# Ranks with layer 0's rows, later layers addressed by rank, one rare branch, two parts per chunk: a four-layer graph network on one core

## The chip, the core and the metric

The kernel runs on one core of one Trainium2 chip. The core has five engines with a queue of instructions each: PE (TensorE, matmuls), DVE (VectorE), ACT (ScalarE), POOL (GpSimd) and SP (SyncE, which issues DMAs); 16 DMA engines move the data that SP and POOL ask for. POOL issues all indirect DMAs: gathers of rows by a column of indices, and scatters. The metric is the device time of one launch in microseconds. Before the change three runs took 5230.04, 5248.34 and 5253.61 us.

## What is computed

3125 nodes of 128 values, 100,000 edges (sorted by destination), and four graph layers, each followed by a residual and a layer norm. Cut to what matters:

```python
x = _layernorm(x + _L0_gnn_ref(x, L0_gnn_z, edge_index, edge_type_500, ...))
x = _layernorm(x + _L1_gnn_ref(x, edge_index, ...))
x = _layernorm(x + _L2_gnn_ref(x, edge_index, edge_attr_3, ...))
x = _layernorm(x + _L3_gnn_ref(x, edge_index, edge_type_8, node_type_4, ...))

# layer 0: attention over edges and the node itself; relation rows z of 500 types
pre_edge = hP1[dst] + hP2[src] + zP3[edge_type]
logit_edge = _leaky(pre_edge) @ y_w
t_edge = hWh[src] + zWz[edge_type]           # weighed by the softmax, summed per dst
# layer 1: mean of neighbours, two matmuls with a relu
# layer 2: softmax over the edges of a node, with a bias from edge_attr
attn = jnp.sum(Q[dst] * K[src], axis=-1) * SCALE + edge_bias
attn_exp = jnp.exp(attn - jnp.max(attn))     # one maximum over all edges
attn_norm = attn_exp / jnp.maximum(attn_sum[dst], 1e-12)
agg = jax.ops.segment_sum(V[src] * attn_norm[:, :, None], dst, num_segments=n)
# layer 3: keys and values by node type, turned by a matrix per edge type (8)
scores = jnp.sum(q_dst * k_t, axis=-1) / scale * mu[edge_type]
out = jax.ops.segment_sum(V[src] * softmax(scores), dst)
```

## The kernel before

**Tiles and slots.** Nodes are padded to 3200 and ranked by falling in-degree (the matmuls `keep`, L325, sort them); tile t holds the 128 nodes of ranks 128t to 128t+127, one to a partition. Each node's incoming edges are its slots; tile t has CAP[t] slots, 57 for the first, 21 for the last, 821 in all. A gather (`gather`, L101) fetches one row per partition: the source node's row for one slot. Slots are worked in chunks of W = 8, 114 chunks in all. Edges beyond CAP are left to `behind` (L773): a `For` loop with `rounds` trips, which is zero trips for these inputs; the function stands ahead of layers 0, 2 and 3.

**Tables in DRAM.** h_tab holds layer 0's rows (1056 bytes, written by 25 stores in order of nodes), kv_tab layer 2's keys and values (1 KB), xq_tab the residual x and query, ktv_tab layer 3's rows, 8 KB a node: one key-value pair for each of 8 edge types. h_tab, kv_tab and ktv_tab lie by node number, xq_tab by rank. A slot's index into the first two is its source's number (`srcx`), into ktv_tab source x 8 + edge type (`idx`, made from `pay[:, :, 2]`).

**Layer 0** is placed by a planner: flows of steps, one per kind of work, are put in an order on each engine. Per chunk, eight gathers bring `hs`; PE transposes and multiplies, ACT applies a relu, DVE sums the logits (L1359) and does the softmax. **Layer 1** multiplies by a table of edge counts on PE, and at its end writes, for each tile j, the rows of kv_tab by a plain store on SP (L1571) and those of xq_tab by a scatter on POOL (L1572).

**Layers 2 and 3** share `passes` (L1678). A beat handles one chunk: the key product of the new chunk (`keyed`, L1593), the weighing of one earlier chunk whose softmax is done, a "part" (`weighed`, L1600), the reduction of the scores (L1596), and the sum over the slots of the part weighed one beat before (`summed`, L1604), which is then added to `accb`. Between these come `lanes.slot()` calls, which run one step each of side lanes: the softmax chain, the closing of a finished tile, the making of its rows, and their put. The order in which the code is written is the order on each engine. In layer 2 a closed tile goes through the output matmuls and yields its 8 KB rows for layer 3 (L1866), which `put3` scatters to ktv_tab by POOL (L104). After the last tile `few` counts the softmax sums that are too small under the global maximum; a branch (L1981) works them anew, which these inputs don't take. Layer 3 begins with memsets of m, l and accb (L2003 to L2006) and its own `behind3`.

Of the kernel before, what the change touches and what calls it, by code (L numbers as in the profile page):

```python
# [9 lines left out]
F32 = mybir.dt.float32  # L10
F16 = mybir.dt.float16
BF16 = mybir.dt.bfloat16
I32 = mybir.dt.int32
# [23 lines left out]
HC = 2 * D + H  # L37
NK = (PADREL + 1) // P
# [48 lines left out]
def tile_gnn(ctx, tc, a, out):  # L87
# [34 lines left out]
    upper = const.tile([P, P], F32, name="upper")  # L122
# [4 lines left out]
    before = const.tile([P, SUP * P], BF16, name="before")  # L127
# [117 lines left out]
    def edge_table(key, unsorted, payload, between):  # L245
# [6 lines left out]
        with tc.tile_pool(name="key_d", bufs=1) as kp, tc.tile_pool(name="kw_d", bufs=3) as kw, \  # L252
# [47 lines left out]
            V.tensor_copy(ranki, rank)  # L300
            rlo = kp.tile([P, NT], I32, name="rlo")
# [45 lines left out]
    h_tab = dram.tile([NP, HC], F32, name="h_tab")  # L347
# [15 lines left out]
    def tables(tp, ps):  # L363
# [12 lines left out]
        def table(src, n, width, w, dst, parts=None):  # L376
            for r in range(0, dst.shape[0], P):
# [13 lines left out]
                if parts is not None:  # L391
                    V.tensor_copy(h[:, HC:], xt)
                    rest = tp.tile([P, R], F32, name="rest")
                    for i in range(3):
                        p = parts[:, r // P, i * R:(i + 1) * R]
                        V.tensor_copy(p, xt if i == 0 else rest)
                        if i < 2:
                            V.tensor_sub(rest, xt if i == 0 else rest, p)
                nc.sync.dma_start(dst[r:r + P], h[:, :dst.shape[1]])
# [4 lines left out]
    with tc.tile_pool(name="edges", bufs=1) as ep:  # L404
# [24 lines left out]
        V.scalar_tensor_tensor(pay[:, :, 2], src, float(NET), et8, op0=OP.mult, op1=OP.add)  # L429
# [456 lines left out]
    with tc.tile_pool(name="l0", bufs=2) as wp, tc.tile_pool(name="l0s", bufs=1) as sp, \  # L886
# [92 lines left out]
        def with_z(hs, s0, k, zs):  # L979
            V.tensor_add(hs[:, s0:s0 + k], hs[:, s0:s0 + k], zs[:, :k, :HC])  # L980
# [20 lines left out]
        def behind0(t, pl, mk, rl):  # L1001
# [3 lines left out]
            hs = wp.tile([P, W, HC], F32, name="hs", bufs=8)  # L1005
# [14 lines left out]
            V.tensor_add(lg, lg_ps, hs[:, :, 2 * D:])  # L1020
# [186 lines left out]
        def flow_rows(k):  # L1207

            yield from hss.take()
            k.hs = wp.tile([P, W, HC], F32, name="hs", bufs=8)  # L1210
# [112 lines left out]
        def add_t(k, s0, n, t_ps):  # L1323
            while k.rows <= (s0 + n - 1) // 4:
                yield 0.5
            V.tensor_add(k.hs[:, s0:s0 + n, D:], k.hs[:, s0:s0 + n, D:], t_ps[:, :n])  # L1326
# [22 lines left out]
        def flow_lg(k):  # L1349
# [9 lines left out]
            V.tensor_add(run.lg[:, at:at + k.w], lg_at[:, run.k % 2, at:at + k.w], k.hs[:, :k.w, 2 * D:])  # L1359
# [81 lines left out]
    with ExitStack() as ctx1, tc.tile_pool(name="l1", bufs=2) as wp, tc.tile_pool(name="l1s", bufs=1) as sp:  # L1441
# [92 lines left out]
        with tc.tile_pool(name="l1pay", bufs=1) as pp:  # L1534
            pays = pp.tile([P, NS, PW], I32, name="pays")
            nc.sync.dma_start(pays.rearrange("p s w -> p (s w)"), pay_tab)
            V.tensor_copy(idx3, pays[:, :, 2])
# [5 lines left out]
        for c in range(NCW):  # L1543
# [12 lines left out]
            for i in range(w // P):  # L1556
# [14 lines left out]
                nc.sync.dma_start(kv_tab[j * P:(j + 1) * P], kv)  # L1571
# [5 lines left out]
    accb = big.tile([P, NT, D], F32, name="accb")  # L1577
    eps = big.tile([P, 1], F32, name="eps")
    V.memset(eps, 1e-5)

# [21 lines left out]
    def summed(pool, kv, n):  # L1602
        u = pool.tile([P, D], F32, name="u", bufs=3)
# [74 lines left out]
    def passes(pool, heads, groups, rows, chain, faded_in, added, finished):  # L1678
# [23 lines left out]
        def beat(key=None, score=None):  # L1702
            part = ready.pop(0) if ready else None
# [3 lines left out]
            if part:  # L1707
                g, kv, w, ex = part
                first = not g.begun
                assert first or g.left == len(g.run) - g.begun or g.begun <= len(g.run)  # L1710
                g.begun += 1
                weighed(kv, w, heads, ex)
# [404 lines left out]
```

## Time and profile before

| what | us |
|---|---|
| median of three runs | 5248.34 |
| the profiled execution's own time | 5237.84 |
| its span | 5236.0 |
| set-up, to the first h_tab gather | 197.7 |
| layer 0, its gathers | 197.7 to 2436 |
| layer 1, to its last scatter | 2440 to 2729 |
| layer 2, its 821 gathers | 2746.8 to 3919.8 |
| layer 2, last put of ktv_tab | 4007.1 |
| layer 3, its 821 gathers | 4020.8 to 5170.2 |
| layer 3, last put of the output | 5230.2 |

Rows of the timeline give the start, the length, the engine, the line, the operation, its output and inputs, and in brackets how long the engine had been idle and what released it. A DMA's row on POOL or SP is its issue alone: the data land later. Rows of the waits give the engine and the instruction that waited, what it waited for, the sum, how many times, and the longest. "issue" is time in which the engine waited for nothing that the profile shows, "remote" a release that it could not trace to an engine. The put of ktv_tab, as a tile:

```
L104 POOL DMA_INDIRECT ktv_tab<-rows,node_d x25: 961/986/1031, 3071.5 to 4007.1; - x25
```

that is 25 instructions, their shortest, mean and longest in ns, and when the first and the last started.

### The profile page before, as it was taken

The page shows a single profiled execution, that of the slowest core. Times are in us where ns is not written, and L with a number is a line of the kernel's source. Part 1 is how long each engine was busy: PE and PEld are TensorE (multiplying, and loading weights), DVE is VectorE, ACT ScalarE, POOL GpSimd, SP SyncE. Part 2 cuts the span into 40 slices and gives each one's busy share as a digit, 9 for nine tenths or more (in the row PEclk, how much of TensorE's full clock was granted, in tenths as well). Part 3 has the DMA queues.
Part 4 walks back from the last instruction along what each step waited for, and adds up shares of the span by engine and source line. Part 5 has one row for each costly group of instructions (what it writes and reads, how often), then busy time and mean ns, then how long its engine had stood idle before and what let it go on. Part 6 is the DMA issues. An engine that isn't in the chain of part 4 may idle for free. (4 is left out here: it accounts for less than half of the span.)

```text
span 5236.0 us, 41120 instructions
## 1 busy us (share of the span) xinstructions
PE 2202.4 (42%) x12631; PEld 1450.8 (28%) x12631; DVE 2941.6 (56%) x6913; ACT 999.5 (19%) x2533; POOL 2723.1 (52%) x2802
## 2 busy tenths in 40 slices
PE   7176777786765777778480022322333000000000
PEld 5154455554544555555230011111111000000000
DVE  8355565665564665665524456556665455554555
ACT  1132233232322333332110011111112000000000
POOL 0524445435334443442217766666662777777774
PEclk9588788788777787888695555555556555555555
DMA  3422233323223222232343333333332333333331
GB/s 83 123 57 78 75 87 87 83 64 91 71 61 89 79 81 79 80 89 73 142 150 105 97 99 104 112 109 114 114 113 86 105 98 93 93 92 93 92 93 50
DMA packets 211921, 482.23 MB, mean 92 GB/s; under 512 B 60713, under 2 KB 110684, under 8 KB 207049
## 3 DMA queue, kind: packets, MB, share of 16 engines
q0 software_dynamic: 130688, 377.49, 25.5%
q1 hardware_dynamic: 80968, 101.69, 6.2%
q8 instruction: 106, 1.74, 0.1%
q14 instruction: 159, 1.30, 0.1%
HBM read 408.43 MB, written 70.63 MB: 91 GB/s over the span
## 5 line engine op out<-in xcount | busy, mean ns | idle before, releaser
L101 POOL DMA_INDIRECT hs<-h_tab,srcx x821 | 830.3, 1011 | 795.3 <-issue 448.8
L101 POOL DMA_INDIRECT kv<-ktv_tab,idx x821 | 852.5, 1038 | 283.2 <-issue 278.4
L101 POOL DMA_INDIRECT kv<-kv_tab,srcx x821 | 781.6, 952 | 357.5 <-issue 254.9
L1593 DVE TENSOR_TENSOR kv<-kv,qp 128x1024 f32<-128x1024 f32 (+4 forms) x228 | 253.2, 1110 | 687.2 <-DMA kv<-ktv_tab,idx 452.4
L1247 PE MATMUL zps<-oh,zq 128*128 128x512 bf16 x1472 | 415.5, 429 | 83.8 <-ACT zT L1252 40.2
L1604 DVE TENSOR_REDUCE u<-kv 128x128 f32<-128x1024 f32 (+4 forms) x228 | 383.8, 1683 | 25.1 <-issue 24.0
L1317 PE MATMUL t_ps<-zw,zT 128*128 128x136 f32 x1472 | 261.4, 315 | 147.2 <-DVE hs L1326 118.0
L1326 DVE TENSOR_TENSOR hs<-hs,t_ps 128x408 f32<-128x408 f32 (+1 forms) x276 | 145.1, 526 | 253.9 <-remote 165.5
L948 PEld LDWEIGHTS pre<-ident,hs 128*128 128x128 f32 x1642 | 244.8, 211 | 137.7 <-issue 132.7
L567 DVE TENSOR_TENSOR c_ohs<-c_ends,c_up 128x1024 bf16<-128x1024 bf16 (+3 forms) x196 | 115.9, 593 | 296.4 <-remote 207.1
L1317 PEld LDWEIGHTS t_ps<-zw,zT 128*128 128x128 f32 x1472 | 217.6, 213 | 170.6 <-issue 79.6
L1596 DVE TENSOR_REDUCE lg<-kv 128x32 f32<-128x1024 f32 (+5 forms) x228 | 251.8, 1104 | 21.7 <-issue 21.4
L948 PE MATMUL pre<-ident,hs 128*128 128x128 f32 x1642 | 250.6, 295 | 29.8 <-issue 28.5
L1600 DVE TENSOR_TENSOR kv<-kv,ex 128x1024 f32<-128x1024 f32 (+4 forms) x228 | 251.3, 1102 | 12.0 <-issue 11.9
L952 PEld LDWEIGHTS lg<-yw,low 128*128 128x128 f32 x1642 | 242.1, 222 | 42.3 <-issue 36.5
L952 PE MATMUL lg<-yw,low 128*128 128x8 f32 x1642 | 238.3, 269 | 28.9 <-issue 27.4
L677 ACT ACTIVATE c_oha<-c_oha,srclo 128x50 bf16<-128x50 bf16 (+2 forms) x821 | 213.0, 347 | 183.0 <-DVE c_oha L567 104.1
L1247 PEld LDWEIGHTS <-zq 128*128 128x128 bf16 x1472 | 157.2, 112 | 265.4 <-issue 163.6
L750 ACT ACTIVATE c_sb<-c_ps 128x512 bf16<-128x512 f32 (+1 forms) x175 | 96.3, 550 | 637.8 <-remote 332.0
L836 PE MATMUL tp<-ident,an 128*128 128x128 f32 x25 | 10.8, 434 | 480.7 <-remote 428.5
L1287 PE MATMUL pre<-zT,zw 128*128 128x512 f32 x368 | 209.3, 652 | 1.9 <-issue 1.8
L567 DVE TENSOR_TENSOR c_ohb<-c_digb,c_up 128x1024 bf16<-128x1024 bf16 (+4 forms) x123 | 73.3, 602 | 241.9 <-remote 112.5
(418 smaller groups left out, 4807.7 us busy)
## 6 DMA issues: line engine op xcount, KB each, us to landing
rb<-rel_tab SPq DMA_DIRECT2D x92, 256.0 KB
c_tab<-c_sb SPq DMA_DIRECT2D x25, 768.0 KB
cs<-c_tab SPq DMA_DIRECT2D x6, 3200.0 KB
hs<-h_tab,srcx POOLq DMA_INDIRECT x821
kv<-kv_tab,srcx POOLq DMA_INDIRECT x821
kv<-ktv_tab,idx POOLq DMA_INDIRECT x821
h_tab<-h SPq DMA_DIRECT2D x25, 132.0 KB
kv_tab<-kv SPq DMA_DIRECT2D x25, 128.0 KB
```

Source lines behind the costliest of these rows:

```text
L101: return G.indirect_dma_start(out=dst, out_offset=None, in_=table, in_offset=indirect(idx), **kw)
L567: V.tensor_tensor(to[:, i // 2:i // 2 + k, :, :w], nums[:, i:i + k * w] .rearrange("p (b w) -> p b w", w=w).unsqueeze(2).to_broadcast([P, ...
L677: A.activation(oha[:, s // 2, 0, :, s % 2], oha[:, s // 2, 1, :, s % 2], AF.Copy, scale=srclo[:, o:o + 1])
L948: T.matmul(pre[:, s, :], hs[:, s0 + s, :D], ident, start=False, stop=(s == k - 1))
L952: T.matmul(lg_ps[:, s, :], low[:, s, :], yw8, start=True, stop=True)
L1247: T.matmul(zps, zq[:, i, 2 * R * k2:2 * R * (k2 + 1)], k.hot[i][:, cols], start=(i + k2 == 0), stop=(i == NK - 1 and k2 == 1))
L1287: T.matmul(pre[:, :n], zw[:, :D], k.zT[:, s0 * P:(s0 + n) * P], start=False, stop=False)
L1317: T.matmul(t_ps[:, s, :], k.zT[:, (s0 + s) * P:(s0 + s + 1) * P], zw[:, D:], start=True, stop=True)
L1593: V.tensor_mul(k, k, qp.unsqueeze(1).to_broadcast([P, n, D]))
L1596: V.tensor_reduce(lg, kv[:, :n, :D].rearrange("p s (h d) -> p s h d", h=heads), AX.X, OP.add)
L1600: V.tensor_tensor(v, v, ex.unsqueeze(3).to_broadcast([P, n, heads, D // heads]), op=OP.mult)
L1604: V.tensor_reduce(u, kv[:, :n, D:].rearrange("p s d -> p d s"), AX.X, OP.add)
```

## The change

- **Ranks.** h_tab's rows grow from 264 to 272 floats (HR); the first of the new columns is the rank of the node, stored by one strided DMA of 3200 single elements, and the rest is zero (25 memsets on POOL). rank_tab is a second table of the same ranks, one column. In layer 0 each gathered row now brings its source's rank, and after a chunk's logits are summed ACT copies the 8 ranks into `srcx` (114 copies); `idx3` becomes rank x 8 + edge type, by one DVE instruction where a copy stood.
- **Tables by rank.** kv_tab's rows are scattered by rank on POOL; layer 2's gathers then use the ranks in `srcx`. ktv_tab's rows lie by rank, so tile t's are 128 rows in one piece and go by a plain store on SP.
- **One rare branch.** `behind2` and `behind3` move into the branch that works layer 2 anew; the condition is now the count of small sums plus `rounds`. `settled`, with the count, is called within `passes` once no group of slots is open, in the written order; before, it came after `passes`. m, l and accb of layer 3 aren't reset at its start (m3 and l3 are set ahead of layer 2).
- **Two parts per chunk.** A beat takes a second part when four or more are ready.

The diff, cut to its core:

```diff
@@ -298,6 +301,9 @@
             V.tensor_copy(ranki, rank)
+            with nc.allow_non_contiguous_dma(reason="3200 ranks, once"):
+                nc.sync.dma_start(h_at[:, :, HC:HC + 1], rank.unsqueeze(2))
+                nc.sync.dma_start(rank_at, rank.unsqueeze(2))
             rlo = kp.tile([P, NT], I32, name="rlo")
@@ -344,7 +350,10 @@
-    h_tab = dram.tile([NP, HC], F32, name="h_tab")
+    h_tab = dram.tile([NP, HR], F32, name="h_tab")
+    rank_tab = dram.tile([NP, 1], F32, name="rank_tab")
+    h_at = h_tab.rearrange("(t p) d -> p t d", p=P)
+    rank_at = rank_tab.rearrange("(t p) d -> p t d", p=P)
@@ -396,12 +405,14 @@
                             V.tensor_sub(rest, xt if i == 0 else rest, p)
+                if parts is None:
+                    G.memset(h[:, HC:HR], 0.0)
                 nc.sync.dma_start(dst[r:r + P], h[:, :dst.shape[1]])
-    with tc.tile_pool(name="edges", bufs=1) as ep:
+    with edges:
         each_of = ep.tile([P, P, CH], BF16, name="each_of")
@@ -426,7 +437,7 @@
         V.tensor_copy(pay[:, :, 1], et)
-        V.scalar_tensor_tensor(pay[:, :, 2], src, float(NET), et8, op0=OP.mult, op1=OP.add)
+        V.tensor_copy(pay[:, :, 2], et8)
         V.tensor_copy(pay.bitcast(F32)[:, :, 3:6], ea)
@@ -1207,7 +1218,7 @@
-            k.hs = wp.tile([P, W, HC], F32, name="hs", bufs=8)
+            k.hs = wp.tile([P, W, HR], F32, name="hs", bufs=8)
@@ -1356,7 +1367,8 @@
             at = k.s0 - run.s0
-            V.tensor_add(run.lg[:, at:at + k.w], lg_at[:, run.k % 2, at:at + k.w], k.hs[:, :k.w, 2 * D:])
+            V.tensor_add(run.lg[:, at:at + k.w], lg_at[:, run.k % 2, at:at + k.w], k.hs[:, :k.w, 2 * D:HC])
+            A.activation(srcx[:, k.o:k.o + k.w], k.hs[:, :k.w, HC], AF.Copy)
             run.to_add -= 1
@@ -1534,7 +1546,7 @@
-            V.tensor_copy(idx3, pays[:, :, 2])
+            V.scalar_tensor_tensor(idx3, srcx, float(NET), pays[:, :, 2], op0=OP.mult, op1=OP.add)
@@ -1568,15 +1580,28 @@
                 A.activation(kv, p_ps[:, D:], AF.Copy)
-                nc.sync.dma_start(kv_tab[j * P:(j + 1) * P], kv)
+                unordered("rows_kv", scatter(kv_tab, ranks[:, j:j + 1], kv), "nodes differ")
                 unordered("rows_xq", scatter(xq_tab, ranks[:, j:j + 1], xq), "nodes differ")
     accb = big.tile([P, NT, D], F32, name="accb")
+    m3 = big.tile([P, NT, 1], F32, name="m3")
+    V.memset(m3, 1e9)
+    l3 = big.tile([P, NT, 1], F32, name="l3")
+    V.memset(l3, 0.0)
+    ktv = ktv_tab.rearrange("n (e f) -> (n e) f", e=NET)
     eps = big.tile([P, 1], F32, name="eps")
     V.memset(eps, 1e-5)
+
+    def ranked(pool, pl):
+        rk = pool.tile([P, W], F32, name="rk", bufs=1)
+        for s in range(W):
+            gather(rk[:, s:s + 1], rank_tab, pl[:, s, 0:1])
+        at = pool.tile([P, W], I32, name="at", bufs=1)
+        V.tensor_copy(at, rk)
+        return at
@@ -1700,26 +1725,27 @@
-            part = ready.pop(0) if ready else None
+            parts = [ready.pop(0) for _ in range(1 if len(ready) < 4 else 2) if ready]
+            later, behind_b[:] = behind_b[:], []
-            if part:
-                g, kv, w, ex = part
-                first = not g.begun
-                assert first or g.left == len(g.run) - g.begun or g.begun <= len(g.run)
+            for i, (g, kv, w, ex) in enumerate(parts):
+                if i and later:
+                    later.pop(0)()
+                    lanes.slot()
+                weighed(kv, w, heads, ex)
+                behind_b.append(lambda g=g, kv=kv, w=w, first=not g.begun:
+                                lanes.add("sum", add_up(g, summed(pool, kv, w), first), 1))
-                weighed(kv, w, heads, ex)
-            if behind_b:
-                behind_b.pop(0)()
-            if part:
-                behind_b.append(lambda: lanes.add("sum", add_up(g, summed(pool, kv, w), first), 1))
+            for done in later:
+                done()
@@ -1737,6 +1763,9 @@
+            if settled and not any(g.open for g in under_way):
+                settled()
+                settled = None
@@ -1763,7 +1792,8 @@
-            kv = rows2(lambda s: pl[:, s, 0:1], W)
+            rk = ranked(wp, pl)
+            kv = rows2(lambda s: rk[:, s:s + 1], W)
@@ -1776,12 +1806,10 @@
-            corr = merged(wp, lg, W, H2, m[:, t, :], l[:, t, :], ex)
+            corr = merged(wp, lg, W, H2, ml[:, t, :], l[:, t, :], ex)
-
-        behind(wp, behind2)
@@ -1869,7 +1897,7 @@
-            put(ktv_tab, od, t, rows.rearrange("p e f -> p (e f)"))
+            nc.sync.dma_start(ktv_tab[t * P:(t + 1) * P], rows.rearrange("p e f -> p (e f)"))
@@ -1953,35 +1981,39 @@
+        f = sp.tile([P, NT, H2], F32, name="f")
+        lf = sp.tile([P, NT, H2], F32, name="lf")
+        fewi = sp.tile([1, 1], I32, name="fewi")
+
+        def shares():
+
+            mx = sp.tile([P, 1], F32, name="mx_all")
+            V.tensor_reduce(mx, ml, AX.XY, OP.min)
+            mt = ps1.tile([P, P], F32, name="tp")
+            T.transpose(mt, mx.to_broadcast([P, P]), ident)
+            top = sp.tile([P, 1], F32, name="top")
+            V.tensor_reduce(top, mt, AX.X, OP.min)
+            A.activation(f, ml, AF.Exp, scale=-1.0, bias=top)
+            V.tensor_mul(lf, l, f)
+
+        def settled():
+            shares()
+            has2 = sp.tile([P, NT, H2], F32, name="has2")
+            V.tensor_scalar(has2, l, 0.0, None, op0=OP.is_gt)
+            V.scalar_tensor_tensor(has2, lf, 1e-12, has2, op0=OP.is_lt, op1=OP.mult)
+            few1 = sp.tile([P, 1], F32, name="few1")
+            V.tensor_reduce(few1, has2, AX.XY, OP.add)
+            few_ps = ps1.tile([1, 1], F32, name="few_ps", tag="tp")
+            T.matmul(few_ps, few1, ones[:, :1], start=True, stop=True)
+            roundf = sp.tile([1, 1], F32, name="roundf")
+            V.tensor_copy(roundf, rounds)
+            V.tensor_add(fewi, few_ps, roundf)
+
-            passes(wp, H2, groups2(), main2, chain2, fade2, add2, finished2)
-
-
-        mx = sp.tile([P, 1], F32, name="mx_all")
-        V.tensor_reduce(mx, ml, AX.XY, OP.min)
-        mt = ps1.tile([P, P], F32, name="tp")
-        T.transpose(mt, mx.to_broadcast([P, P]), ident)
-        top = sp.tile([P, 1], F32, name="top")
-        V.tensor_reduce(top, mt, AX.X, OP.min)
-        f = sp.tile([P, NT, H2], F32, name="f")
-        A.activation(f, ml, AF.Exp, scale=-1.0, bias=top)
-        has2 = sp.tile([P, NT, H2], F32, name="has2")
-        V.tensor_scalar(has2, l, 0.0, None, op0=OP.is_gt)
-        V.tensor_mul(l, l, f)
-        few = sp.tile([P, NT, H2], F32, name="few")
-        V.scalar_tensor_tensor(few, l, 1e-12, has2, op0=OP.is_lt, op1=OP.mult)
-        few1 = sp.tile([P, 1], F32, name="few1")
-        V.tensor_reduce(few1, few, AX.XY, OP.add)
-        few_ps = ps1.tile([1, 1], F32, name="few_ps", tag="tp")
-        T.matmul(few_ps, few1, ones[:, :1], start=True, stop=True)
-        fewi = sp.tile([1, 1], I32, name="fewi")
-        V.tensor_copy(fewi, few_ps)
-        again = nc.values_load(fewi, min_val=0, max_val=NP * H2)
+            passes(wp, H2, groups2(), main2, chain2, fade2, add2, finished2, settled)
+
+        again = nc.values_load(fewi, min_val=0, max_val=NP * H2 + E)
-            V.tensor_scalar(l, l, 1e-12, None, op0=OP.max)
-            rl2 = sp.tile([P, NT, H2], F32, name="rl2")
-            V.reciprocal(rl2, l)
-            V.tensor_mul(f, f, rl2)
@@ -1991,19 +2023,39 @@
             xq_loads()
+            behind(wp, behind2)
+            shares()
+            V.tensor_scalar(lf, lf, 1e-12, None, op0=OP.max)
+            V.reciprocal(lf, lf)
+            V.tensor_mul(f, f, lf)
             for t in range(NT):
+            def behind3(t, pl, mk, rl):
+                kv = wp.tile([P, W, 2 * D], F32, name="kv", bufs=12)
+                at = ranked(wp, pl)
+                V.scalar_tensor_tensor(at, at, float(NET), pl[:, :, 2], op0=OP.mult, op1=OP.add)
+                for s in range(W):
+                    gather(kv[:, s, :], ktv, at[:, s:s + 1])
+                lg = wp.tile([P, 3 * W + 1, H2], F32, name="lg", bufs=4)
+                lg = lg.rearrange("p s h -> p (s h)")[:, :W].unsqueeze(2)
+                keyed(kv, query(ps1, qb[:, t, :], -1.0), W)
+                scored(kv, W, 1, lg)
+                V.tensor_sub(lg[:, :, 0], lg[:, :, 0], mk)
+                ex = ps1.tile([P, 3 * W + 1, H2], F32, name="ex", bufs=2)
+                ex = ex.rearrange("p s h -> p (s h)")[:, :W].unsqueeze(2)
+                corr = merged(wp, lg, W, 1, m3[:, t, :], l3[:, t, :], ex)
+                faded(accb[:, t, :], corr, 1)
+                weighed(kv, W, 1, ex)
+                V.tensor_add(accb[:, t, :], accb[:, t, :], summed(wp, kv, W))
+
+            behind(wp, behind3)
+
             tc.tile_pool(name="l3p", bufs=1, space=PSUM) as ps1:
-        ktv = ktv_tab.rearrange("n (e f) -> (n e) f", e=NET)
-        m = sp.tile([P, NT, 1], F32, name="m")
-        V.memset(m, 1e9)
-        l = sp.tile([P, NT, 1], F32, name="l")
-        V.memset(l, 0.0)
-        V.memset(accb, 0.0)
+        m, l = m3, l3
@@ -2013,20 +2065,6 @@
-
-        def behind3(t, pl, mk, rl):
-            kv = rows3(lambda s: pl[:, s, 2:3], W)
-            lg = wp.tile([P, max(CAP), 1], F32, name="lg", bufs=4)[:, :W]
-            keyed(kv, query3(t), W)
-            scored(kv, W, 1, lg)
-            V.tensor_sub(lg[:, :, 0], lg[:, :, 0], mk)
-            ex = ps1.tile([P, max(CAP), 1], F32, name="ex", bufs=3)[:, :W]
-            corr = merged(wp, lg, W, 1, m[:, t, :], l[:, t, :], ex)
-            faded(accb[:, t, :], corr, 1)
-            weighed(kv, W, 1, ex)
-            V.tensor_add(accb[:, t, :], accb[:, t, :], summed(wp, kv, W))
-
-        behind(wp, behind3)

```

`closing`, `closed`, `typed` and `table3`, which the branch and the lanes call, are as before. u has four buffers instead of three; layer 3's own kv has 14, as before.

More of the change, by code (lines that the diff above doesn't have):

```diff
@@ L37 @@
 HC = 2 * D + H
+HR = HC + 8
 NK = (PADREL + 1) // P
@@ L121, in tile_gnn @@
     V.tensor_copy(onesb, ones)
-    upper = const.tile([P, P], F32, name="upper")
+    edges = ExitStack()
+    ep = edges.enter_context(tc.tile_pool(name="edges", bufs=1))
+    upper = ep.tile([P, P], F32, name="upper")
     G.affine_select(out=upper, in_=ones, compare_op=OP.is_gt, fill=0.0, base=0,
@@ L126, in tile_gnn @@
     V.tensor_copy(upperb, upper)
-    before = const.tile([P, SUP * P], BF16, name="before")
+    before = ep.tile([P, SUP * P], BF16, name="before")
     G.memset(before, 1.0)
@@ L979, in with_z @@
         def with_z(hs, s0, k, zs):
-            V.tensor_add(hs[:, s0:s0 + k], hs[:, s0:s0 + k], zs[:, :k, :HC])
+            V.tensor_add(hs[:, s0:s0 + k, :HC], hs[:, s0:s0 + k, :HC], zs[:, :k, :HC])
         def z_sums(za, zs, w):
@@ L1004, in behind0 @@
             lg_ps = lg_at[:, 0, :W]
-            hs = wp.tile([P, W, HC], F32, name="hs", bufs=8)
+            hs = wp.tile([P, W, HR], F32, name="hs", bufs=8)
             zss = []
@@ L1019, in behind0 @@
             lg = wp.tile([P, 3 * W + 1, H], F32, name="lgs", bufs=3)[:, :W]
-            V.tensor_add(lg, lg_ps, hs[:, :, 2 * D:])
+            V.tensor_add(lg, lg_ps, hs[:, :, 2 * D:HC])
             V.tensor_add(lg, lg, mk.unsqueeze(2).to_broadcast([P, W, H]))
@@ L1325, in add_t @@
                 yield 0.5
-            V.tensor_add(k.hs[:, s0:s0 + n, D:], k.hs[:, s0:s0 + n, D:], t_ps[:, :n])
+            V.tensor_add(k.hs[:, s0:s0 + n, D:HC], k.hs[:, s0:s0 + n, D:HC], t_ps[:, :n])
             tps.give()
@@ L1602, in summed @@
     def summed(pool, kv, n):
-        u = pool.tile([P, D], F32, name="u", bufs=3)
+        u = pool.tile([P, D], F32, name="u", bufs=4)
         V.tensor_reduce(u, kv[:, :n, D:].rearrange("p s d -> p d s"), AX.X, OP.add)
@@ L1676, in __init__, with passes @@
             self.kvs, self.open, self.left, self.begun = [], True, len(run), 0
-    def passes(pool, heads, groups, rows, chain, faded_in, added, finished):
+    def passes(pool, heads, groups, rows, chain, faded_in, added, finished, settled=None):
         lanes, ready = Lanes(), []
```

## The prediction

> **What bounds the kernel now.** I read the slices of the span first, then the windows of the stages, then the groups by line, the waits, and the timeline at each seam between two stages.
>
> ```profile
> span 5236.0 us, 41120 instructions
> PE 2202.4 (42%) x12631; PEld 1450.8 (28%) x12631; DVE 2941.6 (56%) x6913; ACT 999.5 (19%) x2533; POOL 2723.1 (52%) x2802
> POOL 0524445435334443442217766666662777777774
> 200.00:2440.00 2240.00, 1566.66 (x10019) 1112.83 (x10020) 1311.21 (x3718) 684.86 (x1835) 952.51 (x977) 0.80 0.29 80
> 2990.00:3920.00 930.00, 258.67 (x437) 112.73 (x438) 569.07 (x1092) 124.44 (x251) 614.00 (x647) 0.56 0.36 109
> 4240.00:5171.00 931.00, 0.00 (x0) 0.00 (x0) 474.75 (x669) 71.83 (x137) 707.12 (x666) 0.50 0.32 92
> ```
>
> The windows give us, then the busy time of PE, weight loads, DVE, ACT and POOL, the clock, DMA share and GB/s. No engine is busy over 56%, so each stage has its own limit. Layer 0 (200 to 2440) belongs to PE, 70% busy. Layers 2 and 3 are streams of 821 gathers, which POOL issues one by one:
>
> ```profile
> L101 POOL DMA_INDIRECT kv<-ktv_tab,idx x821 | 852.5, 1038 | 283.2 <-issue 278.4
> L101 POOL DMA_INDIRECT kv<-kv_tab,srcx x821 | 781.6, 952 | 357.5 <-issue 254.9
> POOL kv L101 <- remote: 82.1, 24, 12.7
> POOL ktv_tab L104 <- issue: 33.8, 18, 5.7
> DVE kv L1593 <- DMA kv<-kv_tab,srcx: 7.9, 4, 4.0
> ```
>
> The last three lines are waits between 2990 and 3920. In layer 3 POOL waits for nothing but its own 0.3 us of issue: it is the bound. In layer 2 POOL waits 24 times, 82.1 us, for something freed elsewhere, while DVE's key product waits for gathers only 7.9 us: from about 2990 on DVE's chain of steps sets the pace there, and POOL is only nearly full.
>
> **The change, part by part**, against the profiled span of 5236 (that run's own time 5237.8; the median 5248.3 lies 10.5 above it, the three runs span 24).
>
> *Set-up, +5 (0 to 10).* Two columns of 3200 ranks, 4 bytes an element, are stored by SP. The nearest row is a load of 3072 single elements:
>
> ```profile
> 17.11 5.48 SPq L436 DMA_DIRECT2D ntype<-in_node_type  x1
> 127.40 0.25 SPq L382 DMA_DIRECT2D xt<-in_x  x1
> ```
>
> In the built order rank_tab's store stands before the last `xt` load, on which the last x transposes and, behind them on PE, the `keep` matmuls (done at 142) wait; so up to 5.5 us land on the path, 10 if its packets hold the load too. The column of h_tab comes after that load; the first gather of layer 0 is at 197.7, behind 25 gathers and two table builds, which hides it; without that cover it would be another 5.
>
> *Layer 0, +6 (0 to 25).* ACT gets one copy of 128x8 per chunk, 114 in all. Nearby rows of small ACT instructions take 0.20 (128x1) to 0.29 us: 114 x 0.22 = 25 us of ACT time, in a stage where ACT is busy 685 of 2240 us (31%). Nothing is hidden for certain, as ACT's relus feed PE; at ACT's own share, 25 x 0.31, it is 8; I take 6. Rows of 1088 bytes for 1056 cost nothing: gathers are paced by their issue (0.95 + 0.30 us), and DMA is 29% busy. idx3 by one DVE instruction instead of another is even.
>
> *Layer 1 into layer 2, -12 (-9 to -14).*
>
> ```profile
> 2729.00 0.97 POOL L104 DMA_INDIRECT xq_tab<-xq,ranki  x1 [4.93 <-DVE xq L1568]
> 2732.44 3.63 SPq L1583 DMA_DIRECT2D xqb<-xq_tab  x5
> 2746.06 1.28 ACT L1588 ACT_TABLE_LOAD   x1 [16.91 <-DMA xqb<-xq_tab]
> 2746.83 0.99 POOL L101 DMA_INDIRECT kv<-kv_tab,srcx  x1 [16.86 <-issue]
> ```
>
> The first gather comes 17.8 us after the last scatter, though scatters land some 3 us after their issue; it stands behind the `For` of `behind2`, which starts no engine before the 3.3 MB of `xqb` are there. Without the `For`, it waits for the two scatters alone. The kv rows now go by a scatter too: one more POOL issue (0.97 + 0.30) per tile, on a POOL that waits 4.9 us there for DVE, and at the last tile about 3 us with its buffers (0 to 6). So 2732 + 3 = 2735 for 2746.8.
>
> *Layer 2's inside, -10 (0 to -28).* The 25 puts of 1 MB leave POOL's queue for SP. Twenty stand among the gathers: 20 x (0.99 + 0.30) = 26, of which the gathers profit only where they pace. The waits of DVE on gathers over this stretch, all users together, come to 28, my upper bound; since DVE paces, nothing is the lower; I take a third. SP has little else there; the store waits on SP for `rows`, and nothing that others need stands behind it until the branch. The Trainium skill ("DMA: Bandwidth & Descriptors", "Issuing engines are not separate DMA queues") says that moving DMAs to another issuing engine saves only the sequencer's issue time; by it the sum takes the whole 26 if POOL paced and none if DVE does.
>
> *End of layer 2, +4 (0 to 6).* `settled` (minima, a transpose, an exp with 1.28 us of table load, a matmul) moves from behind the last rows into DVE's, ACT's and PE's order at about 3960, where closings run one after the other; its DVE part is some eight short instructions at 0.2 to 0.3, its ACT part 1.3 + 0.4.
>
> *Into layer 3, -7 (-4 to -9).*
>
> ```profile
> 4005.69 0.69 DVE L1866 TENSOR_TENSOR rows<-e_ps,mu 128x512 f32<-128x512 f32 x1 [0.17 <-PE e_ps L1860]
> 4007.13 1.03 POOL L104 DMA_INDIRECT ktv_tab<-rows,node_d  x1 [6.55 <-ACT f L1967]
> 4016.09 0.08 DVE L2003 MEMSET m<- 128x25 f32 x1 [7.75 <-DMA ktv_tab<-rows,node_d]
> 4016.82 2.73 DVE L2006 MEMSET accb<- 128x3200 f32 x1 [0.61 <-issue]
> 4020.79 0.99 POOL L101 DMA_INDIRECT kv<-ktv_tab,idx  x1 [12.63 <-issue]
> ```
>
> From the end of the last rows (4006.4) to the first gather it is 14.4 us: the put's landing (its last packets at 4011.9) and the branch to 4016, a 2.73 us memset, another `For`. One branch stays and the store must land as before; the memset and the second loop go: 14.4 - 7 = 7.4.
>
> *Layer 3, +2.5, then -15 (-8 to -18).* The built order of DVE shows what two parts per chunk do: behind the last key product there stand 7 sums for 12 before; layer 2's order is the same in both. A part costs 1.21 + 1.85 + 0.29 = 3.35 us (L1600, L1604, L2067), and between 5193 and 5227 DVE is nearly solid with such parts. 5 x 3.35 = 17; I take 15, as chains through ACT stay between them. Those five now run inside the stream, where DVE is idle half of the time.
>
> ```profile
> 5170.20 1.09 POOL L101 DMA_INDIRECT kv<-ktv_tab,idx  x1 [0.30 <-issue]
> 5223.87 1.87 DVE L1604 TENSOR_REDUCE u<-kv 128x128 f32<-128x1024 f32 x1
> 5230.16 0.98 POOL L104 DMA_INDIRECT out<-o,node_d  x1 [2.58 <-DVE o L1645]
> ```
>
> But after 4240 gathers that run under a sum (L1604) take 1.29 us, under none 1.00, when one sorts them in the timeline by what DVE does meanwhile. A sum of 1.85 us covers about 1.5 gathers: 0.45 us, so five cost 2.5 (0 to 4.5). The Trainium skill ("SBUF — State Buffer", "Who interferes with whom") says that tensor_reduce never takes the port that VectorE shares with GpSimd; by it these 2.5 are nothing, which this row of layer 3 does not bear out, while layer 2's rows (0.947 under the same sum and under none) do.
>
> *Sum:* 5 + 6 - 12 - 10 + 4 - 7 + 2.5 - 15 = -26.5. From 5238 that is 5211, from the median 5222; I say **5214**.
>
> **Rivals.**
>
> *The puts pay in full.* If POOL paces layer 2 after all, -10 becomes -28, or a little more: 5211 - 18 = 5193. For it: POOL needs 10.0 us for eight gathers, DVE some 10.2 per chunk, almost even. Against: only 7.9 us of waits at the key product.
>
> *The seams pay, the rest is eaten.* Layer 2 yields nothing, and the columns and copies cost their upper bounds: 5238 + 10 + 25 - 12 + 4 - 7 + 2.5 - 15 = 5245, no difference. For it: DVE paces layer 2, and layer 0 is tightly ordered.
>
> *Slower: ACT's copy in layer 0 delays the relus.* ACT works in order; the copy reads the chunk's gathered rows, so its length is not its price if ACT gets to it before they are settled: the next relu waits, then PE. A chunk takes 2240 / 114 = 19.6 us. At 0.6 us more per chunk it is +68 instead of +6: 5211 + 62 = 5273; from 0.6 on the whole is slower. For it: PE is 70% busy, with little slack. Against: the copy stands behind DVE's sum of the logits, which needs the same chunk, and ACT is idle 69% of the time.
>
> *It doesn't do what it says.* The second part needs four ready ones. In layer 2 the order shows none; if in layer 3 the tail is instead kept by ACT's chains (about 5 to 9 us each in the timeline), the -15 goes: 5226.
>
> **How the numbers follow.** Forecast 0.55, puts in full 0.12, eaten 0.20, slower 0.08, no second part 0.05. A measurement of this kernel can tell about 0.5%, 26 us, from no change: faster means below 5222, slower above 5274. The forecast's own range is 5194 to 5234, some 7 parts in 10 of it below 5222; with the first rival that makes 0.54 faster, same 0.37, slower 0.09. All best ends together are 5238 - 69 = 5169, all worst ends 5238 + 24 = 5262; the range 5184 to 5254 leaves out the outer parts.
>
> **What would show it.** Right: the first gather of layer 2 about 6 us after the last scatter, that of layer 3 about 7.5 us after the last rows; about 43 us, not 60, from the last gather to the last put of `out`; layer 2's stream some 10 us shorter, with fewer waits of DVE for kv; layer 0 within 10 us of 2240. Wrong: if layer 0 grows by over 25 us, if the `keep` matmuls end after 155, if the first gather of layer 2 still comes behind the loads of `xqb` (in a wait on a queue's count, say), or if layer 3's gathers take longer than 1.43 us from start to start.

## The result, and the profile after

The changed kernel takes 5218.68 us, the median of 20 runs (5193.69 to 5236.63), the kernel before beside it 5240.6 (20 runs, 5209.31 to 5253.61): 0.9953 of it, 95% interval 0.9940 to 0.9966, so 18 to 31 us less. That is about the 0.5% that the prediction set as its bound, and 5 us from its 5214; the sum of its terms was -26.5, the medians differ by 21.9.

The profiled execution (span 5192.0) is the fastest of those 20 and flatters the change. A later execution of the same kernel, e9 below, has a span of 5209.8 and a time of 5211.47, beside 5240.07 for the kernel before on that chip; it stands nearer to the middle, so both are given; of the kernel before there is one profile. Stages are cut at the first and last gather or scatter of each table and at the end of DVE's last `rows`:

| stage | before | after | e9 | e9 - before | forecast |
|---|---|---|---|---|---|
| set-up, to the first gather of h_tab | 197.7 | 217.8 | 216.9 | +19.3 | +5 |
| layer 0, first to last gather | 2238.3 | 2231.7 | 2240.1 | +1.8 | +6 |
| layer 1 and the way to layer 2's first gather | 310.9 | 301.4 | 299.4 | -11.5 | -12 |
| layer 2, first to last gather | 1172.9 | 1149.6 | 1146.9 | -26.1 | -10 |
| layer 2, last gather to last rows | 86.6 | 78.4 | 93.5 | +6.9 | +4 |
| last rows to layer 3's first gather | 14.4 | 6.1 | 6.2 | -8.2 | -7 |
| layer 3, first to last gather | 1149.4 | 1150.1 | 1150.0 | +0.6 | +2.5 |
| layer 3, last gather to last put | 60.0 | 50.9 | 50.9 | -9.0 | -15 |
| sum of the differences | | | | -26.2 | -26.5 |

The two sums agree, but not term by term. The page of the changed kernel, its first lines, and windows over layer 0, the steady part of layer 2, and layer 3:

```profile
span 5192.0 us, 41675 instructions
...
PE 2208.5 (43%) x12631; PEld 1449.8 (28%) x12631; DVE 2941.3 (57%) x6909; ACT 1016.9 (20%) x2650; POOL 2730.5 (53%) x2827
...
POOL 0434344544433443444236756766662777777774
```

```profile
217.00:2440.00 2223.00, 1555.31 (x9937) 1099.63 (x9937) 1309.63 (x3702) 695.53 (x1938) 950.13 (x972) 0.80 0.29 81
...
2995.00:3900.00 905.00, 260.26 (x445) 113.08 (x445) 572.46 (x1113) 124.65 (x252) 595.81 (x627) 0.56 0.37 113
...
4205.00:5135.00 930.00, 0.00 (x0) 0.00 (x0) 479.11 (x669) 71.98 (x138) 706.38 (x665) 0.50 0.32 92
```

ACT has 117 instructions and 17 us more, POOL 25 instructions and 7 us more, PE 6 us, and DVE is the same within 0.3 us: no engine does less work. In layer 2 the same DVE work (572 us for 569) fits into 905 us instead of 930, and POOL's has shrunk by the puts (596 for 614). What changed is who waits where. The seams, from the timeline:

```profile
126.43 0.41 SPq L306 DMA_DIRECT2D rank_tab<-rank  x1
...
126.96 1.41 SPq L391 DMA_DIRECT2D xt<-in_x  x1
...
143.97 0.45 PE L393 MATMUL xps<-ident,xt 128*128 128x128 f32 x1 [13.62 <-DMA xt<-in_x]
...
2745.88 0.97 POOL L105 DMA_INDIRECT xq_tab<-xq,ranki  x1 [0.80 <-issue]
...
2749.71 3.95 SPq L1608 DMA_DIRECT2D xqb<-xq_tab  x5
...
2750.95 0.99 POOL L102 DMA_INDIRECT kv<-kv_tab,srcx  x1 [2.82 <-issue]
...
3978.27 0.69 DVE L1894 TENSOR_TENSOR rows<-e_ps,mu 128x512 f32<-128x512 f32 x1 [0.17 <-PE e_ps L1888]
...
3979.03 0.32 SPq L1900 DMA_DIRECT2D ktv_tab<-rows  x1
...
3985.07 0.95 POOL L102 DMA_INDIRECT kv<-ktv_tab,idx  x1 [83.49 <-SPq L2016]
...
5135.20 0.95 POOL L102 DMA_INDIRECT kv<-ktv_tab,idx  x1 [0.31 <-issue]
5186.13 0.98 POOL L105 DMA_INDIRECT out<-o,node_d  x1 [2.58 <-DVE o L1670]
```

Layer 2's first gather now starts 5.1 us after the last scatter of xq_tab, at the time of the loads of xqb and not behind them. Layer 3's starts 6.1 us after the last rows. The price stands in the first three rows: the store of rank_tab takes SP 0.41 us only, but the xt load issued right behind it keeps PE waiting for 13.6 us.

### The profile page after: what moved, and what is told of

It is laid out like the page before. It is cut to its first block, busy times and chain, and to the rows that moved or that the text cites. A ratio compares the mean times of both kernels' runs of the same rounds, so it can differ in the third digit from the quotient of the medians.

```text
span 5192.0 us, 41675 instructions
## 1 busy us (share of the span) xinstructions
PE 2208.5 (43%) x12631; PEld 1449.8 (28%) x12631; DVE 2941.3 (57%) x6909; ACT 1016.9 (20%) x2650; POOL 2730.5 (53%) x2827
## 5 line engine op out<-in xcount | busy, mean ns | idle before, releaser
L953 PE MATMUL pre<-identb,hq 128*128 128x512 bf16 (+3 forms) x645 | 196.3, 415 | 9.2 <-issue 8.6
```

Source lines behind the costliest of these rows:

```text
L953: T.matmul(pre[:, :k], hq[:, i, :], identb.unsqueeze(1).to_broadcast([P, k, P]), start=(i == 0), stop=False)
```

## The experiments

Three sets of four, each set on one chip beside the kernel before. The first chip ran the kernel before in 5261.88 us, the second in 4309.57, the third in 5240.07, so times are compared within a set, by their ratio to the kernel before; the stages of the second chip stand apart. The others, and the chip of the result, are called the slower chips.

**e1: rank_tab's store moved into the rare branch.**

```diff
-                nc.sync.dma_start(rank_at, rank.unsqueeze(2))
...
         with tc.If(again > 0):
+            rank_f = sp.tile([P, NT], F32, name="rank_f")
+            V.tensor_copy(rank_f, ranks)
+            with nc.allow_non_contiguous_dma(reason="3200 ranks, once"):
+                nc.sync.dma_start(rank_at, rank_f.unsqueeze(2))
```

> The store of rank_tab (one column, 3200 elements of 4 bytes) moves from the set-up into the rare branch, which these inputs don't take; all else is the changed kernel. In the changed kernel's profile PE stands 13.6 us waiting for the last xt, whose load was issued behind that store, and the keep matmuls end at 159.2 us instead of 142.3. Theory: the 3200 packets of the store hold up the xt load behind them. Then keep ends near 142 to 145, the first gather of layer 0 is at 199 to 203 instead of 217.8, and the whole is 13 to 18 us under the changed kernel (some 40 us under the kernel before). Rival: the later start is due to the wider rows of h_tab, the 25 memsets of them on POOL or the column stored into h_tab; then keep ends near 155 or the first gather is still after 212, and the time is that of the changed kernel within 5 us.

5222.31 us, 0.9929 (0.9904 to 0.9954). The keep matmuls end at 143.0 us, the first gather of layer 0 is at 201.2. SP's rows of e1:

```profile
127.26 0.25 SPq L390 DMA_DIRECT2D xt<-in_x  x1
128.38 6.04 SPq L409 DMA_DIRECT2D h_tab<-h  x7
...
143.64 0.37 SPq L305 DMA_DIRECT2D h_tab<-rank  x1
```

The seven last stores of h_tab take 6.0 us again, for 20.7 in the changed kernel. The theory holds: one store that nothing reads made 16 of the set-up's 19 us; 2 to 3.5 us (201.2 against 197.7, and 199.2 in e12 below) stay with the column in h_tab and the rest. The whole time tells less: by the ratios it is some 13 us under the changed kernel, and the two intervals overlap. The store's own packets are not what took the time. Packets of SP's queue, counted from the traces, with the mean time of one packet of an h_tab row:

```
             changed kernel                       before              e1
us           4-byte packets  h_tab: count, us     h_tab: count, us    h_tab: count, us
126 to 131   2990            360   0.054          734   0.048         762   0.050
131 to 136    279            105   0.713          546   0.048         518   0.050
136 to 141     21            139   0.549            -                   -
141 to 146     25            140   0.187            -                   -
```

The 4-byte packets are nearly all through by 131. Then, for 12 us and more, an ordinary packet behind them takes on the mean 4 to 15 times as long (0.19 to 0.71 us for 0.05). The Trainium skill ("DMA: Bandwidth & Descriptors", "Specifications") says that transfers under 512 bytes make the DMA engine read, modify and write. No trace here shows that step itself; this one shows that the store is dear, and that the price falls on what follows, not on its own packets (0.007 to 0.009 us).

**e2: the puts of ktv_tab on POOL again.**

```diff
+    own_row = big.tile([P, NT], I32, name="own_row")
+    G.iota(own_row, pattern=[[P, NT]], base=0, channel_multiplier=1)
...
-            nc.sync.dma_start(ktv_tab[t * P:(t + 1) * P], rows.rearrange("p e f -> p (e f)"))
+            unordered("rows_ktv", scatter(ktv_tab, own_row[:, t:t + 1], rows.rearrange("p e f -> p (e f)")), "nodes differ")
```

> The 25 puts of ktv_tab go back from SP to POOL, as scatters with a table of row numbers (the same rows, in the same places); all else is the changed kernel. The changed kernel's layer 2, from first gather to last rows, takes 1228.0 us, 31.5 less than before (23.3 among the gathers, 8.2 behind them). Theory: the puts made both; among the gathers POOL's 25 issues of 1.29 us, behind them the scatter's later landing, which keeps the two buffers of rows. Then layer 2 takes 1255 to 1262 us again, and the whole is 20 to 35 us above the changed kernel. Rival: DVE paces layer 2 and the 31.5 us are scatter between executions or come from the addresses by rank; then layer 2 stays within 8 us of 1228 and the whole within 8 us of the changed kernel.

5255.95 us, 1.0000 (0.9982 to 1.0019): the whole gain is gone, some 25 us by the ratios, as expected. Layer 2's gathers take 1177.7 us, its tail 90.0, together 1267.7, above the range expected. The gathers are the clear part: in the eight profiles of slower chips with puts on SP they take 1146.8 to 1155.2 us, with puts on POOL 1172.9 (before) and 1177.7. The tail is not: it takes 78.4 to 96.0 with the puts on SP, 86.6 and 90.0 on POOL, so the expected second part of the theory, a shorter tail, falls. The way into layer 3 is 10.1 us for 5.5 to 6.3: the scatter's last packets land 6.7 us after the end of the last rows, the store's in the changed kernel 4.1.

**e12: the kernel before with that part alone.**

```diff
-            put(ktv_tab, od, t, rows.rearrange("p e f -> p (e f)"))
+            nc.sync.dma_start(ktv_tab[t * P:(t + 1) * P], rows.rearrange("p e f -> p (e f)"))
```

> The kernel before with one part of the change alone: the 25 puts of ktv_tab are plain stores on SP, in order of ranks. Layer 3 still addresses its rows by node number, so it fetches other rows than it should, by equally scattered addresses. Theory: layer 2's gathers take 1149 to 1155 us instead of 1173 to 1178 on a chip where layer 2 waits (25 puts of 1.29 us are 32, of which 23 to 27 show), and 1028 instead of about 1058 on one where the gathers run at 1.25 us; the way from the last rows to layer 3 is 3 to 4 us shorter as the store lands earlier; the whole is 22 to 34 us under the kernel before. Rival: the puts pay only together with the addresses by rank; then it is within 6 us of the kernel before.

5215.66 us, 0.9950 (0.9933 to 0.9968), 24.4 under the kernel before, on the chip where the whole change is worth 29.4. Layer 2's gathers take 1152.1 us, the way into layer 3 is 12.0. One line of the change is worth nearly as much as all of it together, its losses included. The waits of POOL between 3000 and 3935 with the puts on POOL (e2), and, in the second fence, between 2990 and 3895 with them on SP (e12):

```profile
POOL kv L102 <- issue: 183.0, 587, 3.8
POOL kv L102 <- remote: 66.0, 17, 12.7
...
POOL ktv_tab L105 <- issue: 14.8, 16, 5.8
```

```profile
POOL kv L101 <- issue: 186.6, 594, 5.9
POOL kv L101 <- remote: 84.0, 16, 12.7
```

POOL's long waits for the gathers grow from 66 to 84 us when the puts go. With every wait of its gathers except "issue" they come to 116 us in e2 and 102 before, to 127 in e12 and 129 in the changed kernel. The 18 puts in such a stretch hold POOL for 38 us in e2 (18 of their own and 20 of idle time ahead of them), for 52 before (18 and 34). So 10 to 27 us of what is freed becomes waiting, and the stretch is 25 to 30 us shorter (905 for 930 and 935). That this is near 20 issues of 1.29 us is not shown to be their sum. Nor do these runs tell POOL's issues from the scatters' packets, which leave POOL's DMA queue with them.

**e3: the loop of behind2 ahead of layer 2 again.**

```diff
+        behind(wp, behind2)
+
         wo = load(sp, a["L2_gnn_Wo"], "wo")
...
             xq_loads()
-            behind(wp, behind2)
```

> The loop of behind2 (no trips for these inputs) stands ahead of layer 2 again, as in the kernel before; it is taken out of the branch; all else is the changed kernel. Theory: the loop alone holds the first gather behind the loads of xqb. Then the first gather of layer 2 comes 16 to 18 us after the last scatter of layer 1, not 5.1, and the whole is 11 to 13 us above the changed kernel. Rival: the gathers of layer 2 are then just ahead by less and DVE, which paces from about 240 us into the stage, makes up for the later start; then the seam is as long, but the end of layer 2 moves by under 5 us.

5245.97 us, 0.9973 (0.9955 to 0.9992). That is some 10 us above the changed kernel by its ratio of 0.9953, which was taken on another chip; the two intervals overlap, so the seam decides. From e3's timeline:

```profile
2803.61 0.97 POOL L105 DMA_INDIRECT xq_tab<-xq,ranki  x1 [0.30 <-issue]
...
2820.49 1.28 ACT L1613 ACT_TABLE_LOAD   x1 [17.09 <-DMA xqb<-xq_tab]
2821.25 0.99 POOL L102 DMA_INDIRECT kv<-kv_tab,srcx  x1 [15.39 <-issue]
```

The seam is 17.6 us again, POOL waits 15.4 behind the loads of xqb, and the gathers take as long as before it (1149.0). The loop alone made the seam, and nothing later makes up for it.

**e4: one part per beat.**

```diff
-            parts = [ready.pop(0) for _ in range(1 if len(ready) < 4 else 2) if ready]
+            parts = [ready.pop(0)] if ready else []
```

> A beat takes one part again, never two; all else is the changed kernel. Theory: the second part shortens only the tail of layer 3 (last gather to last put), which took 60.0 us before and 50.9 after. Then the tail is 58 to 62 us, the gathers of layer 3 take 1149 to 1151 us as before, layer 2 is unchanged within 5 us, and the whole is 8 to 15 us above the changed kernel. Rival: the sums moved into the stream slow POOL's gathers there, so that taking them out shortens the stream by 3 to 5 us, and the whole is only 4 to 7 us above. Second rival: the tail was shorter by chance or by the cheaper start of layer 3; then it stays near 51.

5248.7 us, 0.9980 (0.9964 to 0.9995), by the ratios some 14 us above the changed kernel. The tail is 60.9 us, in all other profiles of the changed order on the slower chips 50.3 to 50.9; layer 3's gathers take 1149.6 against 1149.9 to 1150.6. So the second part is worth 10 us and costs the stream 0.3 to 0.9. The first rival's 3 to 5 us fall.

**e5, e6: the copies of ranks left out, and made five times.**

```diff
-            A.activation(srcx[:, k.o:k.o + k.w], k.hs[:, :k.w, HC], AF.Copy)
```

> ACT's 114 copies of ranks in layer 0 are left out, so srcx keeps node numbers and layers 2 and 3 fetch other rows than they should, by equally scattered addresses; all else is the changed kernel. Layer 0 took 2238 us in the profile of the kernel before, and 2232, 2246, 2257, 2288 and 2290 in five profiles with the copies, so one profile can't price them and the timed rounds must. Theory: a copy costs 0 to 0.22 us per chunk, and the whole is 0 to 25 us under the changed kernel, most likely 6 to 10. Rival: the copies hold up the relus by 0.3 us and more per chunk; then the whole is 30 us or more under the changed kernel. Second rival: they are hidden, and the two agree within 4 us.

> Each of ACT's 114 copies in layer 0 is made five times (the same copy), 456 more instructions of some 0.2 us, 100 us of ACT time; all else is the changed kernel. Theory (a copy costs its share of ACT's time, about a third of its length): the whole is 25 to 45 us above the changed kernel. Rival 1 (the whole length of each is paid): 90 to 110 us above. Rival 2 (ACT has room for all of it): within 10 us.

4266.13 us without (0.9901) and 4270.13 with five (0.9904). Layer 0 takes 1567.0 and 1568.7 us. The first copy of the five, in e6's groups by line:

```profile
L1371 ACT ACTIVATE srcx<-hs 128x8 int32<-128x8 f32 (+7 forms) x114 | 23.5, 206 | 0.7
```

114 copies are 23.5 us of ACT, as worked out (25), and ACT has room for five times that, as e6 is 4.0 us above e5: rival 2 of e6. For the second rival of e5 the nearest run with one copy is e7 below, 4.2 us above it. Both ran on the second chip, where layer 0 takes 1567 to 1572 us in all four profiles; on the others, where it takes 2230 to 2290, the copy was not tried alone, and there it may not be free. The two profiles without it, the kernel before and e12, have 2238.3 and 2233.5 us; the eight with it have 2231.7 to 2290.4, their median 2247.8, and on the third chip e9 to e11 are 7 to 16 us above e12. One profile each can't settle this, and these kernels also differ in the rows of h_tab.

**e7: settled behind passes.**

```diff
-            passes(wp, H2, groups2(), main2, chain2, fade2, add2, finished2, settled)
+            passes(wp, H2, groups2(), main2, chain2, fade2, add2, finished2)
+        settled()
```

> settled is called once, behind passes, as the count was in the kernel before, not within it; all else is the changed kernel. Theory of the prediction: called early it costs the tail of layer 2 up to 6 us and saves the way from the last rows to the first gather of layer 3 some 2 to 4; called late, the tail is 0 to 6 us shorter (78 to 91 us in the profiles so far) and the seam is 8 to 11 us instead of 6.1, the whole within 6 us of the changed kernel. Rival: the landing of the last store covers the count; then the seam stays at 6 to 7 us and only the tail is shorter.

4270.29 us, 0.9902, within 0.2 us of e6. The seam is 9.9 us for 6.1 and 6.2 in e5 and e6, the tail of layer 2 76.3 for 80.5 and 81.8: what the early count costs the tail, 4 to 5 us, it saves at the seam. The theory holds, with no gain on balance. (e5 and e6 differ from e7 in the copies of layer 0 as well, far from this place.)

**e8 and e11: rank_tab in the branch, and two parts from three ready ones on.**

```diff
-            parts = [ready.pop(0) for _ in range(1 if len(ready) < 4 else 2) if ready]
+            parts = [ready.pop(0) for _ in range(1 if len(ready) < 3 else 2) if ready]
```

> rank_tab's store stands in the rare branch as in e1_rank_in_branch, and a beat takes two parts when three or more are ready, not four; all else is the changed kernel. In the order of DVE 5 sums then stand behind layer 3's last key product, for 7 with four and 12 with one. Theory: the tail of layer 3 is 44 to 48 us (50.9 with four, 60.9 with one: 2.0 us a sum), the set-up ends at 199 to 203, the whole is 16 to 22 us under the changed kernel. Rival: the tail is by then a chain of softmax and closing through ACT; then it stays at 49 to 51 and the gain is that of e1 alone. Second rival: in layer 2 a beat now takes two parts as well and its order is disturbed; then layer 2 is more than 10 us longer than 1228 to 1244.

4254.84 us, 0.9868 (0.9852 to 0.9885), 11 to 15 us under e5, e6 and e7. The first gather of layer 0 is at 196.8 for 210.0 to 211.7, which is all of it; the tail of layer 3 is 29.9 for 30.2 to 30.4. The rival holds there. From the first gather of layer 2 to its last rows it is 1111.9 us for 1104.6 to 1110.4, so the second rival, over 10 us, does not.

> e8_branch_three once more: rank_tab's store in the branch and two parts from three ready ones on. On the faster chip the tail of layer 3 was 29.9 us with five sums left and 30.2 with seven, so nothing was gained there. Theory: where the gathers of layer 3 take 1.4 us from start to start its tail was 50.9 us with seven sums and 60.9 with twelve, and five sums bring it to 46 to 49; where they take 1.28 it stays at 30. So 0 to 4 us under e10_branch_again. Rival: the tail is as long on either chip and the two agree within 2 us.

5201.24 us, 0.9919; its tail is 50.3 us. Five sums instead of seven are worth 0.3 to 0.6 us on the two chips, and the rival holds: below seven, the tail is no longer set by their number.

**e9 and e10: the changed kernel again, and with rank_tab in the branch, on the third chip.**

> The changed kernel as it is, beside the next three on one chip, since the chips of the two calls so far differ (the kernel before took 5262 us on one and 4310 us on the other, where layer 0 takes 1568 us instead of some 2250). Theory: where layer 0 takes about 1570 us, the change is worth 36 to 42 us of some 4310; where it takes 2230 to 2290, 18 to 32 us of some 5250, as layer 0's own scatter lies over it. Rival: the change is worth the same on every chip, 22 to 26 us.

> rank_tab's store stands in the rare branch, as in e1_rank_in_branch; the rest is the changed kernel. Theory: 12 to 17 us under the changed kernel on the same chip. Rival: the gain of e1's profile in the set-up is lost in layer 0; then within 5 us of it.

e9: 5210.67 us, 0.9943 (0.9925 to 0.9961), 29.4 under the kernel before, within the theory's 18 to 32 and above the rival's 22 to 26. e10: 5201.77 us, 0.9922 (0.9902 to 0.9941), 8.9 us less, between its theory (12 to 17) and its rival (5), with 16.1 us less in the set-up and 9.1 more in layer 0, whose time differs by that much between executions (2231.7 to 2290.4 in eight profiles of the slower chips with the copies). The set-up's gain is plain in four profiles; the intervals of the two whole times overlap. e10 and e11 have the lowest ratios to the kernel before on their chip, and e8, with e11's kernel, on the second. The changed kernel itself did not run on the second chip; e5 to e7, which differ from it by 0 to 5 us, are 39 to 43 us under the kernel before there, where e9's theory has 36 to 42.

## Why the prediction was right

The time fell within 5 us of the forecast, but by luck in part: in its sum three terms were wrong by 6 to 16 us, and cancelled. By its steps:

- **Set-up, "+5 (0 to 10)": wrong size, past its upper end.** The place was right (the last xt load behind rank_tab's store, then the keep matmuls). It was priced by SP's issue of a load of 3072 elements; the issue took 0.41 us, and 16 us came from slow packets behind a *store* of single elements (e1). That the packets could hold the load was named as the upper end and sized too small; a load was the wrong neighbour for a store.
- **Layer 0, "+6 (0 to 25)":** +1.8 in e9's account, which is less than layer 0 differs between executions; a price of 7 to 16 us, as between e12 and e9 to e11, is not excluded on the slower chips. The instructions cost ACT what was worked out; they are hidden where that could be tried (e5, e6). The slower rival, +68 by relus that wait, did not come: no profile with the copies is more than 52 us above the kernel before.
- **Layer 1 into layer 2, "-12":** -11.5, by the mechanism named; e3 shows the loop alone.
- **Layer 2's inside, "-10 (0 to -28)": wrong choice.** It measured -23 to -26, near the end that the first rival took. The failing step is "of which the gathers profit only where they pace", with "since DVE paces, nothing is the lower; I take a third". e2 and e12 show 21 to 28 among the gathers, and 24 to 25 in the whole time, with one line turned back, or made alone. The rival's "almost even" misses too: its 10.2 us a chunk for DVE are not DVE's work, rather the spacing of the chunks. Between 2990 and 3920 the 87 key products stand 10.4 us apart on the mean, mostly 6 to 18, and DVE is busy 569 us, 6.5 for each; POOL's gathers there need some 9.0 for each (7.2 of 1.25 us). Neither engine is full, and the few waits at the key product did not show what POOL's queue was worth. DVE's waits for gathers are 22 us before in the list of waits (28 in the prediction) and 14 in the changed kernel, but 23 in e12, which gains as well; by which wait the puts reached the end stays open.
- **End of layer 2, "+4", and the seam, "-7":** +4 to 5 for the tail is what e7 undoes, on the one chip where the tail is steady; elsewhere the tail's 78 to 96 us hide it. The seam is -8.2, near the forecast, but for other reasons. The prediction reckons that "the store must land as before; the memset and the second loop go". e7 gives the early count 3.8 us, and the store on SP is worth 4.0 by e2 and 2.4 by e12; neither is in its term. With the store on SP the way is 12.0 us in e12, which has the memset and the loop, and 9.95 in e7, which has neither and counts as late: the two are worth some 2 us, across two chips.
- **Layer 3, "+2.5":** 0.3 to 0.9 (e4). The rule that was weighed against it, that tensor_reduce does not take the port shared with GpSimd (the Trainium skill, "SBUF — State Buffer", "Who interferes with whom"), fits better than the reading of the row: on the second chip, with the same sums, gathers take 0.95 us under a sum and under none, and only the slower chips stretch them (1.24 and 1.01 us before, from 4240 on).
- **Layer 3's tail, "-15 (-8 to -18)":** -9.0, by the second part (e4: 10.0). Five whole parts of 3.35 us were counted over the whole tail. But for 22 to 23 us after the last gather DVE mostly waits, in either kernel; it is nearly solid from 5193 on before (busy 35.0 of 37 us), from 5157 on after (25.3 of 29), and within that stretch only three whole parts fell away and one of 256 elements, about 11 us, less a reduction of scores (1.2) that now stands in it; DVE's busy time there is 9.7 us less.

Of the two other rivals, "the seams pay, the rest is eaten" was right in that the set-up cost more than its forecast, and wrong in that layer 2 paid as well; "it doesn't do what it says" fell with e4. The chance for faster does not follow from its parts: 0.7 of 0.55 and the rival's 0.12 make 0.505, not 0.54.

## What to carry to other kernels

A strided store of single elements is priced by what stands behind it in the queues, not by its issue; here one column that only a rare branch reads cost the set-up 16 us, and the whole some 9 to 13 us by e10 and e1, whose intervals overlap with the changed kernel's. Where two engines are tied by a ring of buffers and neither is full, a wait list that blamed one did not make the other's instructions free here: take the whole price for what leaves either queue, or both ends as equally likely. To price a tail, count only the work in the stretch where the engine is solid.

## What the runs showed of the hardware

**Two speeds of chip.** On the second chip the kernel before ran in 4309.57 us instead of 5240 to 5262, and the versions of the change in 4255 to 4270 instead of 5201 to 5256. Windows from 600 to 1500 us, the kernel before on the chip of the first runs and then e7 on the second chip:

```profile
600.00:1500.00 900.00, 646.83 (x4148) 461.38 (x4147) 550.53 (x1549) 280.88 (x756) 390.82 (x396) 0.81 0.29 81
```

```profile
600.00:1500.00 900.00, 808.99 (x5826) 592.98 (x5824) 770.62 (x2202) 407.13 (x1148) 589.45 (x560) 0.93 0.42 116
```

In the same 900 us the second chip gets 40 to 52% more of every engine's instructions done, at a granted clock of 0.93 for 0.81. On the slower chips there are stretches such as this one of PE's weight loads in the changed kernel:

```profile
633.43 0.28 PEld L959 LDWEIGHTS pre<-ident,hs 128*128 128x128 f32 x1 [1.81 <-issue]
634.83 0.29 PEld L959 LDWEIGHTS pre<-ident,hs 128*128 128x128 f32 x1 [1.11 <-issue]
636.23 0.29 PEld L959 LDWEIGHTS pre<-ident,hs 128*128 128x128 f32 x1 [1.11 <-issue]
```

They start exactly 1.40 us apart, with no wait that the profile shows, at a granted clock of 0.50 between 622.4 and 637.6; DVE and ACT stand 19 and 21 us meanwhile, put down to "remote". In layer 0, 12 to 27 weight loads follow the one before by 1.40 us in four profiles of the slower chips, none in three of the second. Layer 3's gathers, too, often start 1.40 us apart there (146 of 644 from 4205 on, 308 some 1.25; on the second chip 600 and more are 1.25 apart and at most one 1.40), although PE is idle in that stage. Layer 2's 821 gathers take 1027 to 1029 us on the second chip, 1.25 each. So that DVE paces layer 2, and that layer 3's gathers take 1.43 us from start to start, described the chip as much as the kernel. What holds the engines back was not found; it is no part of the change, but it spreads layer 0 over 2231 to 2290 us and so hides differences of some 10 us in whole times that the stages show plainly.
